# A fused pass with the routed answers added in halves on VectorE, and the gate moved to the next step

## The chip, the cores and the metric

The kernel runs on one core of one Trainium2 chip. The metric is the device time in microseconds of that core, from start to end of one execution; a version is given by the median of its runs. The profile is taken in an execution of its own.

## The reference

The input is 128 graphs of 64 nodes with 256 features, 8192 rows in all. Two layers follow one another, each a graph convolution and a mixture of experts with residuals. The change lies where layer 0 ends and layer 1 begins. Cut to that:

```python
# layer 0, mixture of experts: 64 experts, the best 6 of each row
lattice_out = einsum('bske,bsk->bse', xW, scores)        # sum of 6 weighted answers of a row
proj = lattice_out @ out_w.T + out_b
h = x + proj                                             # x: the normalised row
ffn = (h - mean(h)) * rsqrt(var(h) + 1e-5) * ln_g + ln_b
x = x_before + ffn                                       # x2 in the kernel
# layer 1, graph convolution
h = layer_norm(layernorm(x), ln_gamma, ln_beta)
conv = (adj @ h) @ W_rel + b_rel + h @ W_root
x = x + layernorm(x) + relu(conv)                        # x3 in the kernel
# layer 1, mixture of experts: 8 experts, the best 2 of each row
gate_logits = layernorm(x) @ Wg + bg + bias              # the gate
```

All is in float32; the kernel's tile s holds x + layernorm(x).

## The kernel before

The kernel has four stages: layer 0's convolution and its routing (rows sent to their experts by GpSimd's indirect DMA); layer 0's experts, which send weighted answers to a table in HBM; the fused pass, which reads the six answers of each row back, finishes layer 0, does layer 1's convolution, its gate and its routing; and layer 1's experts.

The fused pass works on blocks of 256 rows (P = 128 partitions, T = 2 tiles of 128 rows, D = 256, K0 = 6 answers, NB = 32 blocks). A helper lays the parts of several blocks one after the other in each step; the pair is a lag and a part, and the part of lag l works on block s - l in step s. Every engine takes its instructions in this order:

```python
        staggered(NB, (
            (-2, load3), (0, layer_out_h), (3, choose1), (-1, mixture), (1, flip_h), (3, count1),
            (2, residual1_a), (0, layer_out_a), (-1, out_proj), (2, residual1_b), (1, neighbours),
            (0, layer_out_b), (1, convolve_a), (2, flip3), (1, convolve_b), (2, gate1), (3, place1),
            (0, layer_out_c), (4, load_w2),
        ))
```

The parts that matter here (cuts marked by ...):

```python
        def load3(b):
            B["y"] = y = work.tile([P, T, K0, D], F32, name="y")          # 2 buffers
            for t in range(T):
                nc.sync.dma_start(out=y[:, t], in_=r0.answer[...])
            # ... xn1, x1, adjacency

        def mixture(b):                       # line 833: sum of 6 answers by accumulating transposes
            pt = psum.tile([P, KD, C], F32, name="ps")
            for t in range(T):
                for k in range(KD):
                    for i in range(K0):
                        nc.tensor.matmul(pt[:, k, ts(t, P)], lhsT=B["y"][:, t, i, ts(k, P)], rhs=ident,
                                         start=(i == 0), stop=(i == K0 - 1), is_transpose=True)
            nc.scalar.copy(accT, pt)          # line 836

        def out_proj(b):                      # line 844: pp = accT.T @ out_wT + out_b
            ...
        def layer_out_h(b):                   # line 850
            nc.vector.tensor_add(h, B["pp"], B["xn1"])

        def layer_out_a(b):
            B["mvh"] = ops.stats(B["h"])      # bn_stats, bn_aggr on VectorE
            B["rsh"] = ops.spread(B["mvh"])   # root on ScalarE
            nc.vector.tensor_add(B["x1"], B["x1"], ln_b...)               # line 856

        def layer_out_b(b):
            nc.vector.reciprocal(rs, rs)
            for t in range(T):                # lines 865 and 867
                nc.vector.scalar_tensor_tensor(h[:, t, :], h[:, t, :], mv[:, t, 0:1], ln_g, subtract, mult)
                nc.vector.scalar_tensor_tensor(x2[:, t, :], h[:, t, :], rs[:, t:t + 1], B["x1"][:, t, :], mult, add)
            B["mv2"] = ops.stats(x2)
            # two roots on ScalarE: std2, rs2

        def layer_out_c(b):                   # VectorE: two reciprocals and shifts; ScalarE: hn (line 884), s
            ...
        def flip_h(b):                        # TensorE turns hn; ScalarE writes hT
        def neighbours(b):                    # TensorE: pz = hT.T @ w_rel; ScalarE copies it to z
        def convolve_a(b), convolve_b(b):     # TensorE: pc = b_rel + hT.T @ w_root, then + at.T @ z

        def residual1_a(b):                   # VectorE: x3 = max(pc, 0) + s, its statistics; ScalarE: root
        def residual1_b(b):                   # VectorE: reciprocal, shift; ScalarE: xs (line 938, written twice wide)
        def flip3(b):                         # TensorE turns xs; ScalarE copies it to xn3T
        def gate1(b):                         # TensorE: pg = xn3T.T @ wg
        def choose1(b):                       # VectorE: logits = pg + bias (line 957), best 2, one-hot
        def count1(b):                        # TensorE: positions from the one-hot
        def place1(b):                        # VectorE: rows of the table; GpSimd: 4 indirect DMAs of xs
```

Of the kernel before, what the change touches and what calls it, by code (L numbers as in the profile page):

```python
# [9 lines left out]
F32 = mybir.dt.float32  # L10
# [5 lines left out]
AF = mybir.ActivationFunctionType  # L16
ALU = mybir.AluOpType
AX = mybir.AxisListType
PSUM = bass.MemoryType.PSUM
P = 128  # L20
# [382 lines left out]
def staggered(n, stages, first=0):  # L403

    for s in range(first + min(lag for lag, _ in stages), n + max(lag for lag, _ in stages)):
        for lag, f in stages:
            if first <= s - lag < n:
                f(s - lag)
# [3 lines left out]
def two_layer_gnn_moe_kernel(ctx: ExitStack, tc: tile.TileContext, a: dict, out: bass.AP):  # L412
    nc = tc.nc
    x_in, adjT = a["x"], a["adjT"]
    N, D = x_in.shape
# [4 lines left out]
    T = 2  # L420
# [5 lines left out]
    K0 = 6  # L426
# [15 lines left out]
    ops = Ops(nc, small, ident, eps)  # L442

    def load_rows(pool, name, engine=nc.scalar):
        t = pool.tile([P, a[name].shape[0]], F32, name="r_" + name)
        engine.dma_start(out=t, in_=rows_of(a[name]))
        return t
# [29 lines left out]
    def by_tile(ap):  # L477
        return ap.rearrange("(t p) d -> p t d", p=P)
# [8 lines left out]
    def load_adjacency(b):  # L487
        at = adjacency[b % 4]
        for g in range(2):
            nc.sync.dma_start(out=at[g * G:(g + 1) * G, :, g * G:(g + 1) * G],  # L490
                              in_=adjT[2 * b * T + g:2 * (b + 1) * T:2].rearrange("t m n -> m t n"))
        return at
# [3 lines left out]
    r0 = Router(tc, const, small, dram, N, D, E0, K0, T, P, 14 * P, 4, "r0")  # L496
# [22 lines left out]
    with tc.tile_pool(name="c0", bufs=1) as c0, \  # L519
# [9 lines left out]
        blocks = [dict() for _ in range(NB)]  # L529
# [263 lines left out]
    with tc.tile_pool(name="c3", bufs=1) as c3, \  # L793
# [5 lines left out]
        ln_g = load_rows(c3, "L0_ffn_ln_g")  # L799
# [11 lines left out]
        blocks = [dict() for _ in range(NB)]  # L811
        pg = pmix.tile([P, T, E1], F32, name="pg")
        r1.begin(counts, work, pmix.tile([P, 2, T, E1], F32, name="pos"))

        def load3(b):
            B = blocks[b]
            B["y"] = y = work.tile([P, T, K0, D], F32, name="y")
            for t in range(T):
                nc.sync.dma_start(out=y[:, t], in_=r0.answer[ts(b * T + t, P * K0), :].rearrange("(p k) d -> p k d", k=K0))
            B["xn1"] = xn1 = work.tile([P, T, D], F32, name="xn1", bufs=3)  # L820
            nc.sync.dma_start(out=xn1, in_=by_tile(xn1_dram[b]))
            B["x1"] = x1 = work.tile([P, T, D], F32, name="x1", bufs=3)
            nc.sync.dma_start(out=x1, in_=by_tile(x1_dram[b]))
            B["at"] = load_adjacency(b)

        def mixture(b):

            B = blocks[b]
            pt = psum.tile([P, KD, C], F32, name="ps")
            for t in range(T):  # L830
                for k in range(KD):
                    for i in range(K0):
                        nc.tensor.matmul(pt[:, k, ts(t, P)], lhsT=B["y"][:, t, i, ts(k, P)], rhs=ident,  # L833
                                         start=(i == 0), stop=(i == K0 - 1), is_transpose=True)
            B["accT"] = accT = work.tile([P, KD, C], F32, name="accT", bufs=1)
            nc.scalar.copy(accT, pt)

# [14 lines left out]
        def layer_out_a(b):  # L852
# [2 lines left out]
            B["rsh"] = ops.spread(B["mvh"])  # L855
            nc.vector.tensor_add(B["x1"], B["x1"], ln_b.unsqueeze(1).to_broadcast([P, T, D]))

        def layer_out_b(b):
            B = blocks[b]
            h = B["h"]  # L860
            mv, rs = B["mvh"], B["rsh"]
            nc.vector.reciprocal(rs, rs)
            B["x2"] = x2 = work.tile([P, T, D], F32, name="x2")
            for t in range(T):
                nc.vector.scalar_tensor_tensor(h[:, t, :], h[:, t, :], mv[:, t, 0:1], ln_g,
                                               op0=ALU.subtract, op1=ALU.mult)
                nc.vector.scalar_tensor_tensor(x2[:, t, :], h[:, t, :], rs[:, t:t + 1], B["x1"][:, t, :],
                                               op0=ALU.mult, op1=ALU.add)
            B["mv2"] = mv = ops.stats(x2)
            B["std2"] = ops.spread(mv)  # L870


            B["rs2"] = rs2 = small.tile([P, T], F32, name="rs2")
            ops.std(rs2, mv[:, :, 1], 1e-10, 1.0 + 1e-5)
# [93 lines left out]
        def place1(b):  # L968
            B = blocks[b]
            r1.send(r1.places(b, B["hot"]), B["xs"])  # L970

        staggered(NB, (
            (-2, load3),
            (0, layer_out_h),
            (3, choose1),
            (-1, mixture),
            (1, flip_h),
            (3, count1),
            (2, residual1_a),
            (0, layer_out_a),  # L980
            (-1, out_proj),
            (2, residual1_b),
            (1, neighbours),
            (0, layer_out_b),
            (1, convolve_a),
            (2, flip3),
            (1, convolve_b),
            (2, gate1),
            (3, place1),
            (0, layer_out_c),  # L990
            (4, load_w2),
# [101 lines left out]
```

## Time and profile before

| | |
|---|---|
| timed runs | 2144.35, 2144.85, 2147.32 us; median 2144.85 us |
| profiled execution, span | 2446.3 us |
| TensorE matmul / weight load busy | 2036.7 us (83%) / 1744.9 us (71%) |
| VectorE, ScalarE, GpSimd busy | 1186.3 us (48%), 1013.6 us (41%), 1157.1 us (47%) |
| fused pass in the profile | about 1480 to 1910 us |
| TensorE / VectorE / ScalarE busy, 1700 to 1800 us | 88.96 / 78.53 / 55.73 us of 100 |
| granted TensorE clock there | 1.00 (0.931 over the whole) |
| DMA share there, and rate | 0.72, 234 GB/s |

PE is TensorE, PEld its weight loads, DVE VectorE, ACT ScalarE, POOL GpSimd and SP SyncE. Shares of the whole span mix four stages; the rows for 1700 to 1800 us are those of the fused pass in its steady part. Busy times of matmuls overlap, since they are pipelined, so that the starts of consecutive matmuls tell their cost better than the durations. The profiled execution is longer than the timed ones by 301 us, which must be kept in mind where a wait is read from the trace.

### The profile page before, as it was taken

How to read it: one execution, taken by the hardware profiler on the slowest of the kernel's cores; microseconds unless marked ns; L12 is line 12 of the kernel's file. 1: busy time of each engine (PE TensorE's matmuls, PEld its weight loads, DVE VectorE, ACT ScalarE, POOL GpSimd, SP SyncE). 2: the span in 40 equal slices, each digit the busy share in tenths (PEclk: the TensorE clock that was granted, in tenths of full speed). 3: DMA queues.
4: the chain of work that ended last, by engine and by line, in shares of the span. 5: the costliest groups of instructions: out<-in, count | busy, mean ns of one | idle time of the engine just before them, and what ended most of it. 6: DMA issues, size and time to landing. Idle time of an engine off the chain costs nothing.

```text
span 2446.3 us, 37355 instructions
## 1 busy us (share of the span) xinstructions
PE 2036.7 (83%) x10564; PEld 1744.9 (71%) x10564; DVE 1186.3 (48%) x3952; ACT 1013.6 (41%) x2037; POOL 1157.1 (47%) x1146
## 2 busy tenths in 40 slices
PE   7888888888884578877878886888888699999998
PEld 6776766767673467766666665777777588888887
DVE  5777776776666322222222234777777222222221
ACT  5766665665662112111111113555555233333332
POOL 0464555455355566666666661333333344444444
PEclk9999989988896799989999998999999799999999
DMA  3233433343236677655555537877773476676665
GB/s 100 90 119 97 132 122 128 123 131 126 88 101 195 199 222 223 203 171 171 178 176 171 146 87 253 300 233 240 232 228 128 141 177 163 156 169 162 161 162 119
DMA packets 284092, 398.93 MB, mean 163 GB/s; under 512 B 56536, under 2 KB 237928, under 8 KB 283888
## 3 DMA queue, kind: packets, MB, share of 16 engines
q1 hardware_dynamic: 204032, 247.67, 34.7%
q0 software_dynamic: 64800, 136.14, 18.7%
q10 hardware_dynamic: 15056, 12.69, 1.6%
q8 instruction: 93, 1.52, 0.3%
q14 instruction: 111, 0.91, 0.1%
HBM read 223.89 MB, written 177.69 MB: 164 GB/s over the span
## 4 chain that ended last, share of the span: by engine, by line
PE 58%; DVE 10%; issue 9%; another core or an unknown queue 8%; ACT 8%; DMA 3%; POOL 2%; SPq 1%; ACTq 0%; POOLq 0%; DVEq 0%
PE py L770 10%; PE ph L1030 9%; PE py L1049 9%; PE ph L599 4%; PE ps L833 3%; PE ps L632 3%; PE pt L755 3%; PE po L844 2%; PE pz L905 2%; PE pc L916 2%; ACT xs L651 2%; ACT lat L602 2%; DVE lat L621 2%; PE ps L76 2%
## 5 line engine op out<-in xcount | busy, mean ns | idle before, releaser
L287 POOL DMA_INDIRECT r0x<-xs,r0row x384 | 390.2, 1016 | 421.0 <-issue 307.1
L770 PE MATMUL py<-lat,pxT 128*128 x1696 | 443.4, 408 | 122.2 <-ACT pxT L757 82.3
L294 POOL DMA_INDIRECT r0y<-py_s,px x424 | 412.5, 973 | 245.9 <-DVE py_s L775 109.9
L770 PEld LDWEIGHTS py<-lat,pxT 128*128 128x128 f32 x1696 | 328.4, 204 | 179.5 <-ACT pxT L757 94.3
L775 DVE TENSOR_SCALAR py_s<-py,px 128x256 f32<-128x256 f32 x424 | 179.5, 478 | 480.0 <-PE py L770 137.8
L302 POOL DMA_INDIRECT out_x<-py_s,px x138 | 214.1, 1551 | 310.1 <-DVE p L1044 124.9
L757 ACT COPY pxT<-pt 128x512 f32<-128x512 f32 x212 | 119.1, 589 | 556.8 <-remote 182.4
L632 PE MATMUL ps<-lat 128*128 128x256 f32 x1024 | 275.7, 420 | 8.3 <-issue 8.0
L1032 ACT ACTIVATE phid<-ph,pw 128x256 f32<-128x256 f32 x276 | 131.0, 475 | 323.8 <-issue 217.4
L632 PEld LDWEIGHTS ps<-lat 128*128 128x128 f32 x1024 | 217.9, 216 | 49.2 <-issue 13.1
L1030 PE MATMUL ph<-pxT,pw 128*128 128x256 f32 x1104 | 252.3, 382 | 0.8 <-ACT pxT L1021 0.8
L1049 PE MATMUL py<-fw,phid 128*128 x1104 | 249.7, 379 | 0.0
L599 PE MATMUL ph<-lat 128*128 128x256 f32 x1024 | 232.8, 386 | 6.8 <-DVE lat L621 6.1
L287 POOL DMA_INDIRECT r1x<-xs,r1row x128 | 126.5, 988 | 226.4 <-DVE bn_rs L881 135.7
L1030 PEld LDWEIGHTS ph<-pxT,pw 128*128 128x128 f32 x1104 | 211.6, 192 | 30.4 <-ACT pxT L1021 1.2
L1049 PEld LDWEIGHTS py<-fw,phid 128*128 128x128 f32 x1104 | 204.5, 190 | 25.0
L599 PEld LDWEIGHTS ph<-lat 128*128 128x128 f32 x1024 | 195.4, 193 | 34.3 <-DVE lat L621 4.8
L755 PE MATMUL pt<-ident,px 128*128 128x128 f32 x848 | 136.3, 285 | 35.4 <-DMA px<-r0x 33.3
L755 PEld LDWEIGHTS pt<-ident,px 128*128 128x128 f32 x848 | 112.5, 148 | 61.9 <-issue 40.5
L602 ACT ACTIVATE lat<-ph,c_L_gnn_b 128x256 f32<-128x256 f32 x256 | 103.9, 470 | 123.4 <-PE ph L599 48.4
L1043 DVE TENSOR_SCALAR p<-p 128x2 f32<-128x2 f32 x69 | 11.9, 173 | 242.3 <-ACT p L1042 238.9
L1052 DVE TENSOR_TENSOR py_s<-py,pb 128x512 f32<-128x512 f32 x69 | 47.7, 692 | 155.6 <-PE py L1049 155.5
(265 smaller groups left out, 2894.5 us busy)
## 6 DMA issues: line engine op xcount, KB each, us to landing
px<-r0x SPq DMA_DIRECT2D x424, 129.0 KB
y<-r0y SPq DMA_DIRECT2D x64, 768.0 KB
pw<-in_L_ffn_W1b SPq DMA_DIRECT2D x69, 514.0 KB
px<-r1x SPq DMA_DIRECT2D x69, 258.0 KB
x<-x SPq DMA_DIRECT2D x64, 256.0 KB
pb<-in_L_ffn_b SPq DMA_DIRECT2D x69, 128.0 KB
r0x<-r0filler ACTq DMA_DIRECT2D x64, 129.0 KB
lat<-in_x SPq DMA_DIRECT2D x32, 256.0 KB
```

Of the source, the lines that this page charges most:

```text
L287: i = self.nc.gpsimd.indirect_dma_start(out=self.table[:, :], out_offset=bass.IndirectOffsetOnAxis(ap=row[:, t, k:k + 1], axis=0), in_=xs[ ...
L294: i = self.nc.gpsimd.indirect_dma_start(out=self.answer[:, :], out_offset=bass.IndirectOffsetOnAxis(ap=x[:, self.D:self.D + 1].bitcast(I32 ...
L302: i, d = f"{self.name}add{i}", self.nc.gpsimd.indirect_dma_start(out=self.total[:, :], out_offset=bass.IndirectOffsetOnAxis(ap=x[:, self.D ...
L599: nc.tensor.matmul(ph[:, c, :], lhsT=w1[:, k, ts(2 * j + c, P)], rhs=B["aggT"][:, k, :], start=(k == 0), stop=(k == KD - 1))
L602: nc.scalar.activation(sq[:, 2 * j + c, :], ph[:, c, :], AF.Square, bias=b1[:, 2 * j + c:2 * j + c + 1], scale=1.0)
L632: nc.tensor.matmul(B["po"][:, t, :], lhsT=B["hT"][:, c, ts(t, P)], rhs=w2[:, c, :], start=False, stop=(t == T - 1 and c == KH - 1))
L755: nc.tensor.transpose(pt[:, k, ts(q, P)], Q["px", q][:, 0, ts(k, P)], ident)
L770: nc.tensor.matmul(py[:, q, :], lhsT=Q["xT"][:, k, ts(q, P)], rhs=lat[:, ds(regs["e"][(2 * j + q) % 4], 1), k, :].rearrange("p o d -> p (o ...
L775: nc.vector.tensor_scalar(y[:, q, :], py[:, q, :], px[:, 0, D + 1:D + 2], None, op0=ALU.mult)
L1030: nc.tensor.matmul(ph, lhsT=w[:, k * F1 + c * P:k * F1 + (c + 1) * P], rhs=Q["xT"][:, k, :], start=(k == 0), stop=(k == KD - 1))
L1032: nc.scalar.activation(hid[:, c, :], ph, AF.Relu, bias=w[:, KD * F1 + c:KD * F1 + c + 1], scale=1.0)
L1049: nc.tensor.matmul(py[:, t, :], lhsT=Q["hid"][:, c, ts(t, P)], rhs=fw2[:, ds(regs["e"][i % 4], 1), c, :].rearrange("p o d -> p (o d)"), st ...
```

## The change

The sum of six answers is formed in two parts: VectorE adds answers 3 to 5 onto answers 0 to 2, in place, two blocks ahead; TensorE's accumulating transposes then run over three instead of six. The load of the answers is a part of its own, one step earlier, with three buffers in place of two. The normalisation of layer 0's output goes from VectorE's fused instructions to two activations of ScalarE, followed on VectorE by one multiplication with ln_g and one addition of x1 for both tiles of rows. The gate's matmuls go from the end of a step to the beginning of the next one; choose follows later on VectorE, after layer_out_a, and count later on TensorE; and in ScalarE's queue the copy that the gate reads stands ahead of the two roots of layer_out_b. The aim is to take transposes from TensorE and to let VectorE's and ScalarE's waits fall together with other work.

```diff
--- before.py
+++ after.py
@@ -812,11 +812,17 @@
         pg = pmix.tile([P, T, E1], F32, name="pg")
         r1.begin(counts, work, pmix.tile([P, 2, T, E1], F32, name="pos"))
 
+        def load_y(b):
+            blocks[b]["y"] = y = work.tile([P, T, K0, D], F32, name="y", bufs=3)
+            for t in range(T):
+                nc.sync.dma_start(out=y[:, t], in_=r0.answer[ts(b * T + t, P * K0), :].rearrange("(p k) d -> p k d", k=K0))
+
+        def halve(b):
+            y = blocks[b]["y"]
+            nc.vector.tensor_add(y[:, :, :K0 // 2, :], y[:, :, :K0 // 2, :], y[:, :, K0 // 2:, :])
+
         def load3(b):
             B = blocks[b]
-            B["y"] = y = work.tile([P, T, K0, D], F32, name="y")
-            for t in range(T):
-                nc.sync.dma_start(out=y[:, t], in_=r0.answer[ts(b * T + t, P * K0), :].rearrange("(p k) d -> p k d", k=K0))
             B["xn1"] = xn1 = work.tile([P, T, D], F32, name="xn1", bufs=3)
             nc.sync.dma_start(out=xn1, in_=by_tile(xn1_dram[b]))
             B["x1"] = x1 = work.tile([P, T, D], F32, name="x1", bufs=3)
@@ -829,9 +835,9 @@
             pt = psum.tile([P, KD, C], F32, name="ps")
             for t in range(T):
                 for k in range(KD):
-                    for i in range(K0):
+                    for i in range(K0 // 2):
                         nc.tensor.matmul(pt[:, k, ts(t, P)], lhsT=B["y"][:, t, i, ts(k, P)], rhs=ident,
-                                         start=(i == 0), stop=(i == K0 - 1), is_transpose=True)
+                                         start=(i == 0), stop=(i == K0 // 2 - 1), is_transpose=True)
             B["accT"] = accT = work.tile([P, KD, C], F32, name="accT", bufs=1)
             nc.scalar.copy(accT, pt)
 
@@ -855,17 +861,19 @@
             B["rsh"] = ops.spread(B["mvh"])
             nc.vector.tensor_add(B["x1"], B["x1"], ln_b.unsqueeze(1).to_broadcast([P, T, D]))
 
+        def layer_out_n(b):
+            B = blocks[b]
+            h = B["h"]
+            rs, nm = ops.scale_shift(B["mvh"], B["rsh"])
+            for t in range(T):
+                nc.scalar.activation(h[:, t, :], h[:, t, :], AF.Identity, bias=nm[:, t:t + 1], scale=rs[:, t:t + 1])
+
         def layer_out_b(b):
             B = blocks[b]
             h = B["h"]
-            mv, rs = B["mvh"], B["rsh"]
-            nc.vector.reciprocal(rs, rs)
             B["x2"] = x2 = work.tile([P, T, D], F32, name="x2")
-            for t in range(T):
-                nc.vector.scalar_tensor_tensor(h[:, t, :], h[:, t, :], mv[:, t, 0:1], ln_g,
-                                               op0=ALU.subtract, op1=ALU.mult)
-                nc.vector.scalar_tensor_tensor(x2[:, t, :], h[:, t, :], rs[:, t:t + 1], B["x1"][:, t, :],
-                                               op0=ALU.mult, op1=ALU.add)
+            nc.vector.tensor_mul(h, h, ln_g.unsqueeze(1).to_broadcast([P, T, D]))
+            nc.vector.tensor_add(x2, h, B["x1"])
             B["mv2"] = mv = ops.stats(x2)
             B["std2"] = ops.spread(mv)
 
@@ -970,22 +978,25 @@
             r1.send(r1.places(b, B["hot"]), B["xs"])
 
         staggered(NB, (
+            (-3, load_y),
             (-2, load3),
+            (3, gate1),
             (0, layer_out_h),
-            (3, choose1),
             (-1, mixture),
             (1, flip_h),
-            (3, count1),
             (2, residual1_a),
             (0, layer_out_a),
+            (3, choose1),
             (-1, out_proj),
             (2, residual1_b),
+            (0, layer_out_n),
             (1, neighbours),
-            (0, layer_out_b),
+            (3, count1),
+            (-2, halve),
             (1, convolve_a),
             (2, flip3),
+            (0, layer_out_b),
             (1, convolve_b),
-            (2, gate1),
             (3, place1),
             (0, layer_out_c),
             (4, load_w2),
```

## The prediction

> **What bounds the kernel now.** I first looked for the stage that the diff touches. The instructions of tile y (the answers that the fused pass reads back) run from 1484 us to 1869 us of the profiled span, so the fused pass takes roughly 1480 to 1910 us of 2446 us. It is cut into steps, one block of 256 rows entering in each; the start of the 24 transposes of line 833 marks a step. The timeline of two stretches gives the step length:
>
> ```profile
> 1512.58 2.78 PE L833 MATMUL ps<-ident,y 128*128 128x128 f32 x24
> ...
> 1515.45 0.59 ACT L836 COPY accT<-ps 128x512 f32<-128x512 f32 x1 [2.01 <-PE ps L833]
> ...
> 1516.09 1.99 PE L844 MATMUL po<-m_L_ffn_out_wT,accT 128*128 128x256 f32 x8
> ```
>
> ```profile
> 1523.78 2.81 PE L833 MATMUL ps<-ident,y 128*128 128x128 f32 x24
> ...
> 1526.69 0.59 ACT L836 COPY accT<-ps 128x512 f32<-128x512 f32 x1 [1.90 <-PE ps L833]
> ...
> 1535.07 2.82 PE L833 MATMUL ps<-ident,y 128*128 128x128 f32 x24
> ...
> 1539.85 0.59 ACT L836 COPY accT<-ps 128x512 f32<-128x512 f32 x1 [3.77 <-PE pos L191]
> ```
>
> ```profile
> 1662.86 2.82 PE L833 MATMUL ps<-ident,y 128*128 128x128 f32 x24
> ...
> 1667.15 0.59 ACT L836 COPY accT<-ps 128x512 f32<-128x512 f32 x1 [3.29 <-PE pos L191]
> ...
> 1667.79 1.99 PE L844 MATMUL po<-m_L_ffn_out_wT,accT 128*128 128x256 f32 x8 [1.36 <-ACT accT L836]
> ```
>
> Columns: start us, duration, engine and line, tiles, and in brackets the idle time before it and what ended it. Read the first column. In the first two steps shown TensorE goes from one mixture to the next in 11.20 us (1512.58 to 1523.78) and 11.29 us (1523.78 to 1535.07), almost without waiting: the copy of the mixture starts 0.1 us after the last transpose ends. Later (1650.16, 1662.86, 1675.53) a step takes 12.7 us, and the difference is one wait: the copy starts some 1.4 us after the transposes end (1665.68), and TensorE stands for it. The wait appears with the step of 1535 us, the first in which GpSimd sends rows by indirect DMA. The waits of the stretch 1500 to 1868 us, 29 steps, say the same (waiter, what it waited for, us in total, times, longest):
>
> ```profile
> ACT accT L836 <- PE pos L191: 86.9, 26, 3.8
> ...
> PE po L844 <- ACT accT L836: 37.5, 27, 1.8
> ...
> DVE logits L957 <- PE pg L951: 29.8, 25, 1.4
> ...
> DVE bn_rs L67 <- ACT bn_sd L36: 21.1, 27, 1.3
> ```
>
> Nothing in the program makes this copy wait for more than its transposes. The profiled execution took 2446 us and the timed ones 2145 us, so some 300 us of what the trace shows is absent from the timed runs. I take this late signal to belong to it (chance 0.8): in a timed run **TensorE bounds the fused pass at about 11.25 us a step**, and VectorE is close behind. All waits of VectorE in that stretch, with the small ones, come to 57.4 us, or 1.98 us a step, so it is occupied 12.68 - 1.98 = **10.7 us a step**, of which 11.25 leaves about half a microsecond.
>
> **What the Trainium skill says.** "VectorE: DVE Perf Modes", section "The perf-mode tier table": an fp32 tensor_tensor runs at one element a cycle only; section "The TRN2 errata" gives (N+151)/0.96 ns, 691 ns for 512 elements. The trace agrees: 659 ns with both inputs in SBUF (line 856), 691 ns with one in PSUM (line 850). "Perfetto Trace Analysis", section "Per-engine timelines", says that a matmul's end is modelled from its size; so I trust starts, and the 1.4 us rests on the copy's start as well. "TensorE: Matmul & The Clock Gate", section "PE-mode transpose", says that transposes don't count as TensorE work to the clock gate in the same way; the clock was 1.00 in this stretch with 32 transposes a step, so no run here shows what thinner work does.
>
> **The change, part by part.** The rows that carry the costs (groups of 1540 to 1868 us; the numbers behind the bar are busy us and mean ns of one):
>
> ```profile
> L833 PE MATMUL ps<-ident,y 128*128 128x128 f32 x617 | 72.5, 274 | 0.0
> ...
> L938 ACT ACTIVATE xs<-x,bn_nm,bn_rs 128x512 f32<-128x512 f32 x52 | 39.6, 810 | 7.7 <-issue 6.2 <-POOL xs L249 1.2 <-DVE bn_nm L68 0.2
> ...
> L884 ACT ACTIVATE hn<-x,bn_nm,bn_rs 128x256 f32<-128x256 f32 x52 | 28.3, 594 | 0.0
> ...
> L867 DVE SCALAR_TENSOR_TENSOR x<-h,bn_sd,x 128x256 f32<-128x256 f32 x52 | 25.2, 485 | 1.8
> ...
> L865 DVE SCALAR_TENSOR_TENSOR h<-h,bn_mv,r_L_ffn_ln_g 128x256 f32<-128x256 f32 x52 | 24.6, 473 | 0.0
> ...
> L856 DVE TENSOR_TENSOR x<-x,r_L_ffn_ln_b 128x512 f32<-128x512 f32 x26 | 17.1, 659 | 0.0
> ```
>
> - TensorE: 12 of 24 transposes go. 24 take 2.65 us start to start (1662.86 to 1665.51), so this is -1.32 us a step. TensorE without its waits goes from some 11.1 to 9.8 us.
> - VectorE, halving: one add of 1536 elements. From the 659 ns of 512 and one element per cycle of 0.96 GHz (the clock on the "VectorE: DVE Perf Modes" page, section "Specifications") I estimate 659 + 1024/0.96 = 1726 ns, and 1.64 us of occupation, because an independent instruction starts some 0.08 us before the end of the one ahead of it (as at line 867 to 865).
> - VectorE, output norm: four instructions of 473 and 485 ns (1.83 us start to start, 1656.55 to 1658.38) become a multiply and an add of 512, dependent on each other, 2 x 0.69 = 1.38 us, and one 0.16 us instruction for the shift. Together VectorE gets +1.64 - 1.83 + 1.38 + 0.2 = +1.4 us: **12.1 us of occupation**, above TensorE's 11.25.
> - ScalarE: two activations of 256, 1.09 us a step as at line 884 (pair). It has room, but they stand behind the two of line 938 in its queue.
> - Gate at the next step's begin: choose no longer waits for it (1.2 us a step in the profile, half of that in a step of 11.25). In the new order choose, 1.58 us, stands between the statistics and the reciprocals and so covers the roots (0.73 us).
> - The third buffer and earlier load of y: the same bytes; TensorE waited for y only in the first steps (22 us in 7 waits), so worth little.
>
> Then a new wait. VectorE's multiply needs h from ScalarE. In VectorE's order the shift of x3 releases the two activations of line 938 (1.52 us for the pair, of which the second lets go after 0.70 us each, 1.40 us) and behind them the two new ones (1.08 us); with two handovers h is ready 2.6 us after that shift. VectorE meanwhile has 0.3 us of small work and the halving, some 1.95 us, and stands 0.65 us. A step along VectorE, from starts in the step of 1662.86 us: h add 0.61; x3, two sets of statistics and the x1 add 3.44; choose 1.58; reciprocal and shift 0.36; until h is there 2.61; multiply and add 1.38; statistics of x2 1.08; places, reciprocals and shifts 1.71. The sum is **12.77 us**. The length of the halving doesn't enter; it lies within the 2.61.
>
> **The total.** 12.77 - 11.25 = +1.5 us a step. It applies where choose, norm and mixture all run, about 29 of 36 steps: +43 us. In the first steps, without choose and place, VectorE has 2.5 us less and the new kernel may gain up to a microsecond each; say -2 us. 2145 + 41 = 2186 us. I shade it to 2182 for the rival.
>
> **Rivals.**
> 1. The late signal is real in timed runs also. Then the step before is 12.68 us, VectorE's 12.77 us replaces it and the late copy falls into TensorE's new slack: +3 us, about 2148. For it: it recurs in every step. Against it: the 300 us between profile and timing have to be somewhere, and the same kind of late TensorE signal is seen in the stages with the most GpSimd sends. Chance 0.2.
> 2. TensorE's relief is what counts and VectorE keeps up: a step of about 10 us, -35 us. The 10.7 us of VectorE before the change and the +1.4 us speak against it; it needs the fp32 add at twice its rate and no wait for h. Chance 0.02.
> 3. TensorE, with 3 us of idle time in each step, is granted a lower clock, and its chain from hn over hT, pz and z to pc gets longer than the slack of about 0.7 us; a few tenths a step more, 2190 to 2200. No idle stretch above 1.5 us is expected, so a minor share.
> 4. DMA: its share of 0.72 at 12.68 us is about 0.81 at 11.25 us, so the pass before may be somewhat slower than 11.25 us in timed runs; then the loss shrinks by a few us.
>
> **Range and chances.** The first reading gives 2176 to 2197, the first rival 2140 to 2155. A range for 8 in 10 must hold both: 2142 to 2198. Slower by over 2% starts at 2187.7, about the middle of the main case with the third rival added: 0.43. Faster by over 2% needs rival 2 in full: 0.02. Within 2% is left with 0.55.
>
> **What the profile after would show.** VectorE's halving at about 1.73 us; its waits for logits and roots nearly gone, and one for h of about 0.65 us before the multiply; TensorE idle some 3 us a step; the step in the profile about 12.7 to 12.8 us, hardly other than before, so that the profiled span stays near 2446 us while the timed runs grow. If the profiled step stays and the timed runs stay too, the late signal was no matter of profiling and rival 1 holds. If the halving takes clearly less than 1.7 us, my rate for it is wrong, without effect on the step. The prediction fails most if VectorE has no wait for h, or if the timed step before is not 11.25 us.

## The result and the profile after

The changed kernel takes **2201.07 us** (four runs, 2198.19 to 2203.2), the kernel before in the same comparison 2144.6 us (2143.31 to 2147.32). The ratio is 1.0261, 95% interval 1.0243 to 1.0279: the change costs 56.5 us. The profiled execution of after has a span of 2201.4 us, as long as its timed runs, so its trace can be read without correction. TensorE's matmuls are busy for 1921.6 us (2036.7 before), VectorE 1231.6, ScalarE 1044.1, GpSimd 1162.8 us: TensorE is busy 115 us less, and the kernel is slower.

On some of the chips used the kernel before takes about 2484 us, with TensorE's signals coming late as in the profile of before, and on the others about 2147 us as in the timed runs, so each experiment is compared only with the kernel before on its own chip. I call them late chips and prompt chips.

First a step of after, in the timeline (VectorE and a few lines of the others; start us, duration):

```profile
1403.35 1.52 ACT L946 ACTIVATE xs<-x,bn_nm,bn_rs 128x512 f32<-128x512 f32 x2 [2.12 <-DVE bn_rs L67]
1403.45 1.76 DVE L822 TENSOR_TENSOR y<-y 128x1536 f32<-128x1536 f32 x1
1404.77 1.07 ACT L869 ACTIVATE h<-h,bn_nm,bn_rs 128x256 f32<-128x256 f32 x2
1405.88 0.69 DVE L875 TENSOR_TENSOR h<-h,r_L_ffn_ln_g 128x512 f32<-128x512 f32 x1 [0.67 <-ACT h L869]
...
1408.15 1.51 PE L839 MATMUL ps<-ident,y 128*128 128x128 f32 x12
...
1416.29 1.76 DVE L822 TENSOR_TENSOR y<-y 128x1536 f32<-128x1536 f32 x1
...
1420.99 1.51 PE L839 MATMUL ps<-ident,y 128*128 128x128 f32 x12
```

From halving to halving (1403.45 to 1416.29) and from mixture to mixture (1408.15 to 1420.99) it is **12.84 us**. VectorE stands once in a step: after the halving it waits 0.67 us for h, because ScalarE first writes the two halves of xs (1403.35) and only then h (1404.77). The waits of the stretch 1240 to 1600 us say the same (waiter, awaited, us in total, times, longest):

```profile
PE ps L76 <- ACT hn L892: 22.4, 47, 2.5
...
DVE h L875 <- ACT h L869: 18.0, 27, 0.9
```

No wait for logits is left, and that for roots is 3.8 us in 5 times. TensorE now waits for others in every step. In 1400 to 1500 us (us, busy times of PE, PEld, DVE, ACT, POOL, clock, DMA share, GB/s) VectorE is the fullest engine:

```profile
1400.00:1500.00 100.00, 85.90 (x491) 70.28 (x489) 88.36 (x346) 60.47 (x131) 31.41 (x38) 0.97 0.71 231
```

The other part is the beginning of the pass. Its timeline in after:

```profile
1213.36 0.34 SPq L818 DMA_DIRECT2D y<-r0y  x1
...
1230.02 0.17 DVE L808 TENSOR_TENSOR r_L_ffn_bg<-r_L_ffn_bg,r_L_ffn_bias 128x8 f32<-128x8 f32 x1 [15.17 <-DMA r_L_ffn_bias<-in_L_ffn_bias]
...
1230.77 3.43 DVE L822 TENSOR_TENSOR y<-y 128x1536 f32<-128x1536 f32 x2 [0.51 <-DMA y<-r0y]
...
1232.63 2.79 PE L839 MATMUL ps<-ident,y 128*128 128x128 f32 x12 [48.69 <-DMA xn<-xn]
```

and in the profile of before:

```profile
1478.31 0.34 SPq L819 DMA_DIRECT2D y<-r0y  x1
...
1484.05 2.79 PE L833 MATMUL ps<-ident,y 128*128 128x128 f32 x12 [17.28 <-DMA y<-r0y]
...
1491.98 0.17 DVE L808 TENSOR_TENSOR r_L_ffn_bg<-r_L_ffn_bg,r_L_ffn_bias 128x8 f32<-128x8 f32 x1 [11.63 <-DMA r_L_ffn_bias<-in_L_ffn_bias]
```

Before, the first mixture starts 5.7 us after the first load of answers is issued, and the tiny addition of the gate's bias (line 808), which waits for a transfer, comes later and holds up nothing. After, the first mixture starts 19.3 us after the load: it needs the halving, the halving stands behind line 808 in VectorE's queue, and line 808 waits 15.17 us for its bias. Line 808 starts 16.7 us after the load of answers, in before 13.7 us; why the bias comes later isn't shown.

### The profile page after: what moved, and what is told of

Read it like the earlier page. It is cut to its first block, busy times and chain, and to the rows that moved or that the text cites. A ratio compares the mean times of both kernels' runs of the same rounds, so it can differ in the third digit from the quotient of the medians.

```text
span 2201.4 us, 36751 instructions
## 1 busy us (share of the span) xinstructions
PE 1921.6 (87%) x10180; PEld 1649.8 (75%) x10180; DVE 1231.6 (56%) x3952; ACT 1044.1 (47%) x2101; POOL 1162.8 (53%) x1146
## 3 DMA queue, kind: packets, MB, share of 16 engines
q10 hardware_dynamic: 15056, 12.69, 1.8%
## 4 chain that ended last, share of the span: by engine, by line
DMA 32%; PE 25%; DVE 21%; POOL 8%; issue 8%; ACT 6%; ACTq 0%; SPq 0%; POOLq 0%; DVEq 0%
DMA r0y<-py_s,px 17%; PE py L1060 8%; PE ph L1041 8%; POOL r0x L287 6%; DMA out_x<-py_s,px 5%; DVE bn_st L45 3%; DMA r0x<-xs,r0row 3%; DMA r1x<-xs,r1row 3%; PE py L770 2%; DVE lat L609 2%; DMA px<-r0x 2%; PE ph L599 2%; DVE lat L621 2%; ACT xs L946 1%; DVE bn_mv L46 1%
## 5 line engine op out<-in xcount | busy, mean ns | idle before, releaser
L287 POOL DMA_INDIRECT r0x<-xs,r0row x384 | 395.6, 1030 | 256.4 <-issue 171.7
L770 PE MATMUL py<-lat,pxT 128*128 x1696 | 409.6, 385 | 40.3 <-DVE py_s L775 23.6
L775 DVE TENSOR_SCALAR py_s<-py,px 128x256 f32<-128x256 f32 x424 | 185.6, 480 | 362.3 <-PE py L770 150.8
L770 PEld LDWEIGHTS py<-lat,pxT 128*128 128x128 f32 x1696 | 306.7, 191 | 90.4 <-ACT pxT L757 32.7
L757 ACT COPY pxT<-pt 128x512 f32<-128x512 f32 x212 | 123.8, 585 | 429.7 <-PE pt L755 281.1
L632 PE MATMUL ps<-lat 128*128 128x256 f32 x1024 | 237.6, 381 | 0.0
L632 PEld LDWEIGHTS ps<-lat 128*128 128x128 f32 x1024 | 193.4, 191 | 24.4
L755 PE MATMUL pt<-ident,px 128*128 128x128 f32 x848 | 127.9, 274 | 37.1 <-DMA px<-r0x 37.1
L755 PEld LDWEIGHTS pt<-ident,px 128*128 128x128 f32 x848 | 106.4, 142 | 58.5 <-issue 37.3
L623 ACT ACTIVATE lat<-lat,c_L_gnn_rms_weight 128x256 f32<-128x256 f32 x256 | 105.6, 495 | 36.9 <-DVE lat L621 36.5
```

Source lines behind the costliest of these rows:

```text
L287: i = self.nc.gpsimd.indirect_dma_start(out=self.table[:, :], out_offset=bass.IndirectOffsetOnAxis(ap=row[:, t, k:k + 1], axis=0), in_=xs[ ...
L632: nc.tensor.matmul(B["po"][:, t, :], lhsT=B["hT"][:, c, ts(t, P)], rhs=w2[:, c, :], start=False, stop=(t == T - 1 and c == KH - 1))
L755: nc.tensor.transpose(pt[:, k, ts(q, P)], Q["px", q][:, 0, ts(k, P)], ident)
L757: nc.scalar.copy(xT[:, :, :n * P], pt[:, :, :n * P])
L770: nc.tensor.matmul(py[:, q, :], lhsT=Q["xT"][:, k, ts(q, P)], rhs=lat[:, ds(regs["e"][(2 * j + q) % 4], 1), k, :].rearrange("p o d -> p (o ...
L775: nc.vector.tensor_scalar(y[:, q, :], py[:, q, :], px[:, 0, D + 1:D + 2], None, op0=ALU.mult)
```

## The experiments

My theory after this reading had two parts: the step is VectorE's queue with its wait for h (12.84 us against 11.3 us before on a prompt chip), and the bias delays the beginning. The rivals were that the step before is 12.7 us in timed runs too, so that the loss lies elsewhere; that the halving itself sets the step; and that the changed place of the gate does.

### What the step before is in a timed run

The kernel before, unchanged, was profiled again on two late chips (three executions):

> The kernel before, profiled once more. Theory A (the late TensorE signals of the first profile belong to that execution and not to the timed runs): the span falls to about the timed 2145 us, the copy of the mixture starts 0.1 us after its last transpose, and a step of the fused pass takes 11.2 to 11.3 us. Theory B (the late signal is part of the program): the step stays at 12.7 us and the span near 2446 us.

> The kernel before once more, profiled, hoping for an execution in which TensorE's signals are not late (the earlier run of it took 2473 us and showed them again). Theory A: where the whole takes about 2145 us, the copy of the mixture starts 0.1 us after its last transpose and a step of the fused pass takes 11.2 to 11.3 us. Theory B: the step is 12.7 us there also.

> The kernel before, profiled, complete with its sends. Theory A: where it takes about 2145 us, the step is 11.29 us as without the sends, and between 2470 and 2490 us it is 12.8 us.

They took 2472.93, 2480.26 and 2480.65 us and have steps of 12.79, 12.78 and 12.78 us. The waits of the second, 1560 to 1900 us:

```profile
ACT accT L836 <- PE pos L191: 78.4, 23, 3.5
```

ScalarE stands 3.4 us a step ahead of the copy. In the step of 1704.84 us the next matmul starts at 1707.49 us, so the transposes are through by about then, and the copy starts at 1709.21 us, 1.7 us later; the program doesn't make it wait for the matmul named, line 191. So the late copy of the mixture is the same as in the first profile. The timed runs on these chips are as long as the profiled ones (medians of 2483.86, 2484.27 and 2482.17 us), so the late copy belongs to the chip or its condition, not to profiling. It is the smaller part of what a late chip costs: the first answers are loaded at 1495.6 to 1504.5 us there and at 1212.9 us on a prompt chip (e8, below), so that 283 to 292 of the 337 us arise ahead of the fused pass, in stages that no run here changed.

The traces tie the late copy to GpSimd's sends. In the profile of before and in these three, it starts 0.1 us after the transposes in the two steps ahead of the first send, and in each of 107 later steps it starts 0.8 to 1.3 us after the end of the last of the step's four sends. One step with sends has no late copy, that of 1577.80 us in e1b: its last send ends at 1579.52 us, 1.1 us before its transposes do. It and the next step, in the timeline of e1b (DMA_INDIRECT is a send, the fourth of its step):

```profile
1578.55 0.97 POOL L287 DMA_INDIRECT r1x<-xs,r1row  x1 [0.31 <-issue]
...
1580.71 0.59 ACT L836 COPY accT<-ps 128x512 f32<-128x512 f32 x1 [1.90 <-PE ps L833]
...
1591.93 0.97 POOL L287 DMA_INDIRECT r1x<-xs,r1row  x1 [0.30 <-issue]
...
1593.98 0.59 ACT L836 COPY accT<-ps 128x512 f32<-128x512 f32 x1 [3.88 <-remote]
```

To find whether the sends cause it, the sends of layer 1's rows were left out of the kernel before and of after. Both then leave out layer 1's experts' real input and read filler rows instead; the work of the other engines stays.

```diff
-            r1.send(r1.places(b, B["hot"]), B["xs"])
+            r1.places(b, B["hot"])
...
-            r1.fetch(i, row, x)
+            nc.sync.dma_start(out=x, in_=r1.table[ds(r1.spare, r1.pg), :].rearrange("(t p) d -> p t d", p=P))
```

> The kernel before without GpSimd's sends of the fused pass; layer 1's experts then read the page of fillers, so that their part is left out of the output. TensorE's late signals went with GpSimd's sends in the traces so far. Theory A: without sends there is no late signal in the fused pass on any chip, and its full step, choose and place included, takes 11.2 to 11.3 us. Theory B: the 12.7 us belong to the step, and it stays there.

> The changed kernel without GpSimd's sends of the fused pass, layer 1's experts on fillers, as in the run beside it. Theory A with C: the step is set by VectorE and ScalarE, 12.8 us with sends and without, so 1.5 to 1.6 us longer than that of the kernel before without sends. Theory B: both are at 12.7 to 12.8 us.

> The changed kernel itself, timed beside the kernel before on whatever chip this call gets. Theory A: where the kernel before takes about 2145 us, ratio 1.026; where it takes about 2484 us, its step is 12.8 us as the changed one's and only the beginning (some 10 us) is lost, ratio 1.003 to 1.007. Theory B: ratio 1.026 there also.

> The kernel before without GpSimd's sends of the fused pass, layer 1's experts on fillers, once more. On a chip where the kernel before takes 2484 us: Theory A, the late signals of the fused pass go with the sends and its step falls from 12.8 to 11.3 us. Rival: they come from something else, such as the loads, and the step stays at 12.8 us. On a chip where it takes 2145 us: 11.29 us again.

All four ran on prompt chips, where the kernel before takes 2148.15 and 2149.81 us. Without sends, before took 2176.21 and 2183.69 us and after 2232.0 us (one execution each; from the last hn to the end they take 588 us and more, against 560 in after, and in that stage they read the fillers). After unchanged took 2203.96 us, ratio 1.0263 (1.0246 to 1.028). So whether a late chip without sends has no late copy was not tested. But e8 and g1 show what I had wanted more, the step before without late signals, 11.29 us in every full step. A stretch of the timeline of e8:

```profile
1395.94 2.82 PE L833 MATMUL ps<-ident,y 128*128 128x128 f32 x24
...
1398.85 0.59 ACT L836 COPY accT<-ps 128x512 f32<-128x512 f32 x1 [1.90 <-PE ps L833]
...
1407.24 2.82 PE L833 MATMUL ps<-ident,y 128*128 128x128 f32 x24
```

The copy follows the transposes at once and TensorE doesn't wait for it; from 1265 to 1590 us TensorE is busy for 321.26 of 325 us. After has 12.73 us without and 12.83 us with sends, and the difference e9 - e8 is 55.8 us, the same as the change costs with its sends in both kernels (55.8 us, 2203.96 - 2148.15). That the sends add little to the step before on a prompt chip follows from this agreement, to within several us only, since g1 took 7.5 us more than e8; a trace of it with sends on a prompt chip wasn't taken.

The loss is therefore located with e8 against after, and with e8 against e9, where both are without sends. The tile hn, written once for each block at the end of its output norm, gives the first and last start (duration min/median/max, first to last start):

```profile
L884 ACT ACTIVATE hn<-x,bn_nm,bn_rs x64: 584/594/604, 1240.3 to 1586.8; 128x256 f32<-128x256 f32 x64
```

```profile
L892 ACT ACTIVATE hn<-x,bn_nm,bn_rs x64: 582/593/608, 1248.1 to 1641.7; 128x256 f32<-128x256 f32 x64
```

The first answers are loaded at 1212.9 us in e8 and at 1213.4 us in after, which gives

| us | first load to first hn | first to 4th hn | 4th to 32nd hn | chip |
|---|---|---|---|---|
| before without sends (e8) | 27.4 | 30.4 | 315.6 | prompt |
| after | 34.7 | 33.6 | 359.5 | prompt |
| difference | +7.3 | +3.2 | +43.9 | |
| after without sends (e9) | 35.6 | 34.1 | 356.7 | prompt |
| difference of e9 and e8 | +8.2 | +3.7 | +41.0 | |

Together +54.4 of 56.5 us; about 2 us lie elsewhere. Without sends in either it is +52.9 of 55.5 us between the profiled spans; the rest is 1.3 us ahead of the first load and 1.2 us behind the last hn. So the full steps cost 41 to 44 us. The first column is the least certain: g1, the same kernel as e8, has 29.1 us there. The last of the three steps in the second column is a full one, since the first choose runs in it (1273.35 us in after): it takes 12.69 us in after and 11.30 us in e8, so that 1.4 of the 3.2 us belong to the full steps, 29 in all.

### The bias of the gate moved out of the way

```diff
-        nc.vector.tensor_add(bg, bg, gbias)
...
         def choose1(b):
+            if b == 0:
+                nc.vector.tensor_add(bg, bg, gbias)
```

> The changed kernel, with the addition of the two gate biases moved from ahead of the fused pass to its first choose. Theory P (at the beginning the first halving stands in VectorE's queue behind this addition, which waits 15 us for the DMA of a bias, and TensorE waits for the halving): the fourth mixture comes some 8 to 11 us earlier, the time falls from 2201 to about 2191 us, steps unchanged at 12.84 us. Rival Q (the first mixture is late because three blocks of answers share the DMA engines): no change, 2200 us.

> The changed kernel with the bias addition late. The first profile of it showed the fourth mixture 7 us sooner after the first load of answers than in the changed kernel. Theory P: 7 us less than the changed kernel, ratio about 1.023 where the kernel before takes 2145 us. Rival Q (those 7 us are given back later): ratio 1.026.

On two late chips: 1.0032 (1.0019 to 1.0045) and 1.0031 (1.0013 to 1.005), step 12.84 us. The beginning, in the timeline of e2:

```profile
1505.90 0.34 SPq L817 DMA_DIRECT2D y<-r0y  x1
...
1515.11 1.76 DVE L821 TENSOR_TENSOR y<-y 128x1536 f32<-128x1536 f32 x1 [7.65 <-DMA m_L_gnn_W_root<-in_L_gnn_W_root]
...
1516.97 2.79 PE L838 MATMUL ps<-ident,y 128*128 128x128 f32 x12 [19.17 <-DMA m_L_ffn_Wg<-in_L_ffn_Wg]
```

The first halving starts 9.2 us after the load of answers in place of 17.4, the first mixture 11.1 in place of 19.3, and the fourth 38.1 in place of 45.4 us: 7 us are kept. Line 808 is their cause, and rival Q (no change) is out. After was traced on a prompt chip and e2 on a late one, but e11 below, on a prompt chip, has 11.1 and 39.0 us too. Of the rest of the delay of the first mixture (11.1 less the 5.7 of before), nearly all goes with the halving (next experiment, 6.3 us). What the 7 us are worth in a timed run wasn't measured on one chip: after wasn't timed on a late chip, nor e2 on a prompt one. These ratios mustn't be held against 1.0261, since the kernel before is held up by its late copy on these chips.

### Six transposes again, no halving

```diff
-                    for i in range(K0 // 2):
+                    for i in range(K0):
-                                         start=(i == 0), stop=(i == K0 // 2 - 1), is_transpose=True)
+                                         start=(i == 0), stop=(i == K0 - 1), is_transpose=True)
...
-            (-2, halve),
```

> The changed kernel without the halving: TensorE transposes six answers again, all else as changed. Theory C (a step is set by the chain of VectorE through ScalarE's xs and h, in which the halving lies hidden): VectorE loses 1.64 us of work a step and the step still takes 12.7 to 12.8 us, its wait for h growing from 0.67 to about 2.4 us; the time falls only by what the beginning gives back, to some 2190 us. Rival D (VectorE's load is what counts, and the halving is the added load): the step falls to about 11.2 to 11.5 us and the time to 2150 to 2155 us.

> The changed kernel without the halving. Its steps were 12.84 us in the first profile of it. Theory C: the time falls only at the beginning and end, 8 to 14 us under the changed kernel, ratio 1.020 to 1.023 where the kernel before takes 2145 us. Rival D (load): ratio 1.005.

> The changed kernel without the halving, once more, for a chip where the kernel before takes 2145 us. Theory C: ratio 1.020 to 1.023 there. Rival D (load): ratio 1.005. Elsewhere 1.002 again.

Late chips: 1.0005 (0.9989 to 1.0021) and 1.0021 (1.0009 to 1.0033). Prompt chip: 2193.2 us, **1.0207** (1.019 to 1.0224). The step is 12.84 us on both, exactly that of after, although VectorE has 1.76 us less work and TensorE 12 more transposes. The timeline of g2:

```profile
1398.54 0.69 DVE L875 TENSOR_TENSOR h<-h,r_L_ffn_ln_g 128x512 f32<-128x512 f32 x1 [2.35 <-ACT h L869]
...
1400.81 2.81 PE L839 MATMUL ps<-ident,y 128*128 128x128 f32 x24
...
1413.64 2.82 PE L839 MATMUL ps<-ident,y 128*128 128x128 f32 x24
```

The wait for h grew from 0.67 to 2.35 us, by what the halving had filled. The granted clock is 1.00 in 1400 to 1500 us, against 0.97 in after, so the clock doesn't make the step either. In after the halving is free; undoing it gains only at the beginning. There the first mixture starts 6.3 us after the load, and the first hn comes 25.6 us after it (34.7 in after): 9.1 us of some 11 us (2193.2 against 2203.96 us for after in another comparison on a prompt chip).

### The norm ahead of xs in ScalarE's queue

If the wait for h is the second part of the loss, putting the two activations of the output norm ahead of those of xs removes it, and VectorE's own work is left.

```diff
-            (2, residual1_b),
             (0, layer_out_n),
+            (2, residual1_b),
```

> The changed kernel with the normalisation of layer 0's output ahead of the two wide activations of xs, on VectorE and ScalarE. Theory C: the wait of 0.67 us for h goes, and with it 0.7 to 0.9 us of each step, which takes 11.9 to 12.2 us; 29 steps make 19 to 26 us, so about 2175 to 2182 us. Rival D (load alone): the load is the same, so no change, 2200 us.

> The changed kernel with both mends: norm of layer 0's output ahead of xs, bias addition late. Steps of 12.08 us and 7 to 10 us less at the beginning: some 30 us below the changed kernel. Where the kernel before takes about 2145 us that is still above it, ratio 1.011 to 1.014; where it takes 2484 us, ratio 0.991 to 0.995.

e4, on a late chip: 0.9961 (0.9946 to 0.9975), step 12.08 us. e11, with the bias moved as well, on a prompt chip: 2172.08 us, 1.0122 (1.01 to 1.0143), step 12.07 us; it is 32 us faster than after in the same comparison. The timeline of e4:

```profile
1709.72 1.09 ACT L869 ACTIVATE h<-h,bn_nm,bn_rs 128x256 f32<-128x256 f32 x2 [2.19 <-DVE bn_rs L67]
1709.82 1.76 DVE L822 TENSOR_TENSOR y<-y 128x1536 f32<-128x1536 f32 x1
...
1711.50 0.69 DVE L875 TENSOR_TENSOR h<-h,r_L_ffn_ln_g 128x512 f32<-128x512 f32 x1
...
1723.57 0.69 DVE L875 TENSOR_TENSOR h<-h,r_L_ffn_ln_g 128x512 f32<-128x512 f32 x1
```

The multiplication follows the halving without a wait, and from one to the next it is 12.07 us: now VectorE is hardly ever idle (0.9 us in all, from 1560 to 1900 us), and this is its occupation. In e11 the first hn comes 27.5 us after the load, as before the change (27.4), and first to last hn take 370.7 us (393.6 in after): 7.2 + 22.9 us, nearly the whole 32. TensorE needed 11.29 us with 12 transposes more, so VectorE is the bound now; and as 12.07 us is above 11.29 us, this form of the change doesn't win on a prompt chip. No run has the norm first and no halving, which would show whether TensorE's 11.29 us would then limit the step again.

### The output norm back on VectorE

Only the halving, the earlier load and the gate's place are left of the change; layer_out_n is taken out and layer_out_b is the old one.

```diff
-            nc.vector.tensor_mul(h, h, ln_g.unsqueeze(1).to_broadcast([P, T, D]))
-            nc.vector.tensor_add(x2, h, B["x1"])
+            for t in range(T):   # the two scalar_tensor_tensor of before, after nc.vector.reciprocal(rs, rs)
...
-            (0, layer_out_n),
```

> The changed kernel with layer 0's output norm back on VectorE in its four fused instructions; halving, gate and queue order as changed. Theory C: the wait for h is gone, VectorE's chain is 0.61 + 3.44 + 1.58 + 0.36 + 0.08 + 1.64 + 1.83 + 1.08 + 1.71 = 12.3 us, so a step of 12.2 to 12.4 us against 12.84; over 29 steps some 15 us less than the changed kernel, so about 1.9% above the kernel before where that takes 2145 us. Rival (the gain of the norm's move outweighs its wait): a step above 12.84 us.

> The changed kernel with the norm back on VectorE. Its steps were 12.25 us in the first profile of it: 29 times 0.59 us less than the changed kernel, with the first steps some 20 us, ratio 1.016 to 1.018 where the kernel before takes 2145 us.

Late chips: 0.9961 (0.9946 to 0.9977) and 0.9976 (0.9963 to 0.9989), steps 12.25 and 12.24 us. VectorE stands 0.7 us in all from 1560 to 1900 us in e5, so this too is its occupation. Moving the norm to ScalarE therefore made the step 0.6 us longer in the order of after, and 0.17 us shorter with the norm first. It wasn't run on a prompt chip; by its step, 12.25 against 11.29 us, I would expect it above before there, but no run shows it.

### The gate's place alone, and the halving on GpSimd

The kernel before with the stage order of the gate, choose and count from after:

```diff
+            (3, gate1),
-            (3, choose1),
-            (3, count1),
             (0, layer_out_a),
+            (3, choose1),
...
-            (0, layer_out_b),
+            (3, count1),
             (1, convolve_a),
             (2, flip3),
+            (0, layer_out_b),
             (1, convolve_b),
-            (2, gate1),
```

> The kernel before with only the new order: gate at the next step's begin, choose after layer_out_a, the gate's copy ahead of the roots of layer_out_b; no halving, the norm as before, two buffers of answers. Theory C: TensorE's load is unchanged at 11.1 us, VectorE's 10.7 us; a step of 11.1 to 11.3 us, a ratio of 0.995 to 1.003 where the kernel before takes 2145 us. Rival (the order itself costs, because choose and the copy delay the roots): a step of 11.6 us or more, ratio above 1.005.

On a late chip: 1.0000 (0.9984 to 1.0016), step 12.78 us. The late copy of the mixture still sets the step there (TensorE waits for it 37.4 us in 25 times from 1560 to 1900 us), so this tells nothing of a prompt chip; whether the order alone gains or loses there isn't shown. The waits of VectorE were exchanged, not removed: for logits they are gone, and those for the two roots come to 50.2 us in 32 times in that stretch. In after the waits for logits and roots are nearly gone, but choose, 1.59 us, now stands on VectorE ahead of the shift that releases xs and so h. Its place is thus a part of the chain that leads to the wait for h, and no run moves it alone out of after; with that wait gone (e4) the step is 12.08 us all the same.

The halving on GpSimd, with the norm of before and the bias moved:

```diff
-            nc.vector.tensor_add(y[:, :, :K0 // 2, :], y[:, :, :K0 // 2, :], y[:, :, K0 // 2:, :])
+            nc.gpsimd.tensor_add(y[:, :, :K0 // 2, :], y[:, :, :K0 // 2, :], y[:, :, K0 // 2:, :])
```

> The changed kernel with the halving given to GpSimd, the norm back on VectorE and the bias addition late. GpSimd is busy for a third of the stage; VectorE's load is then 10.7 us and TensorE's 9.8 us. Theory C: if GpSimd adds 1536 elements in under 5 us and does not slow VectorE, a step of 10.5 to 10.9 us and a ratio of 0.98 to 0.99 against the kernel before of 2145 us. Rival: GpSimd's adds are so slow, or take so much of VectorE's time at the memory, that the step is 11.5 us or more.

On a late chip: 1.0017 (0.9999 to 1.0035), with a median step of 12.26 us but a mean of 12.95 us; the 10.5 to 10.9 us of theory C are missed, as its rival said. GpSimd's addition takes 3433 ns. VectorE loses what it gave away; its groups in 1560 to 1900 us (busy us, mean ns of one):

```profile
L861 DVE TENSOR_TENSOR x<-x,r_L_ffn_ln_b 128x512 f32<-128x512 f32 x26 | 45.3, 1744 | 0.0
...
L181 DVE CAST r1which<-r1idx 128x4 f32<-128x4 uint32 x26 | 31.5, 1210 | 0.9
```

In e5 the same two take 658 and 170 ns. In e7 itself, the 16 additions of line 861 that overlap one of GpSimd's take 2421 ns in the mean and the other 10 take 661 ns; of the conversions, 9 overlap and take 3173 ns, and 17 don't and take 170 ns.

## Why the prediction was wrong

The prediction said 2182 us and 2142 to 2198 us for 8 in 10; 2201.07 us lies 3 us above the range. The mechanism was right: the step is VectorE's queue with its wait for h. What was mis-sized is the term for the first steps.

- **The step before, 11.25 us:** 11.29 us without sends on prompt chips. Right.
- **VectorE's sum, 12.77 us:** 12.84 us. In the trace of after the terms are, from h's addition: 0.60, 3.43, 1.59, 0.36, 2.61, 1.45, 1.09, 1.71. Only the multiplication and addition differ, 1.45 in place of 1.38 us: each takes 0.69 us, but the one that needs the other's result starts 0.73 us after it (1405.88 and 1406.61). The wait for h is 0.67 us (0.65 said).
- **"The length of the halving doesn't enter":** shown by g2, whose step without any halving is 12.84 us. The halving takes 1758 ns by the median of 32, against the 1726 of the estimate, which started from the 659 ns of line 856; (1536+151)/0.96 of the Trainium skill, "VectorE: DVE Perf Modes", section "The TRN2 errata", gives 1757 ns.
- **VectorE's occupation, 12.1 us:** 12.08 and 12.07 us, in e4 and e11 where the wait is gone.
- **+43 us from the full steps:** +43.9 us over 28 steps and +1.4 us in one more; without sends in either kernel 41.0 and 1.4. Right.
- **"In the first steps ... say -2 us":** this is the step that failed. The traces have +9.1 us there: 7.3 us until the first hn (5.6 us against g1) and 1.8 us in the next two steps. I had counted what VectorE has to do in these steps and not where the first halving stands in its queue: behind an addition whose operand arrives late. Both could be seen beforehand: the 11.63 us wait of line 808 in the profile of before, and the halving's place behind it in the listing. e2 and e11 show 7 us to be that: in e11 the first hn comes 27.5 us after the load, in before 27.4. The sentence that the load of y was "worth little" looked at TensorE's wait for y (22 us in 7 waits) and missed that the halving needs every half of y ahead of the first transpose. The two steps behind it are no shorter in g2 and e11 (21.6 and 21.2 us against 20.9 in after and 19.1 in e8), so neither the halving, nor the bias, nor the norm's place in the queue makes them longer; the cause stays open.
- **Shading by 4 us, and the low end of the range:** they served rival 1, the late signal as a matter of timed runs also. Rival 1 is a fact on late chips and isn't one where the kernel is timed at 2145 us. The reason given against it, that the signal belongs to the profiled execution, was wrong, since late chips have it in timed runs as well; that the timed runs of 2145 us are free of it was right, and with it the 11.25 us. The same error made the forecast that the profiled span would stay near 2446 us: it is 2201.4 us. Without the shading and with the right beginning the same sum is 2145 + 43 + 9.1 = 2197.1 us.
- **Rival 2** (VectorE keeps up) falls with g2 and e11. **Rival 3:** the clock did go down, from 1.00 to 0.97 in the stretch 1400 to 1500 us, and TensorE's waits in the step from 1408.15 us are 0.78 + 0.17 + 0.69 + 0.63 = 2.3 us (3 said), but g2 at 1.00 has the same step of 12.84 us. **Rival 4** (DMA slows the step before) isn't seen in e8, whose sends are left out and whose DMA share is 0.62; with sends it wasn't tested.

## What to carry to other kernels

Before work is moved to another engine, write down that engine's queue from end to end, waits included: the step was predicted within 0.07 us in this way, and a halving that costs nothing in a full step cost 7 us once, since its first instance stood behind an unrelated instruction waiting for a transfer. An in-order queue makes the first steps of a pipeline a case of their own: look for what a newly critical engine still waits for there. Where the profiled execution is longer than the timed ones, find what the extra time is made of before choosing which of its waits to believe.

## What the runs showed of the hardware

- The same kernel takes about 2147 us on some chips and 2484 us on others, 16% more. In the fused pass the difference of a step is the copy that starts about 1.5 us after the transposes end (11.29 and 12.78 us). So the verdict on a change depends on the chip: the order with the norm first, whose step is 12.07 to 12.08 us on both, is 0.4% faster than before on a late chip and, with the bias moved, 1.2% slower on a prompt one. After itself wasn't timed on a late chip. On late chips the late copy goes with GpSimd's sends (it starts 0.8 to 1.3 us after the end of the last of them); why on these chips alone stays open. The profile of before, with its 2446 us, looks like one from a late chip, and which chip it was isn't known.
- An addition of 1536 fp32 elements takes GpSimd 3433 ns and VectorE 1758 ns. The Trainium skill, "GPSIMD Engine Reference", section "Instruction dispatch", gives approximately 2.5 cycles an element as the floor for two inputs, at its 1.2 GHz an estimate of 3200 ns; the trace lies 7% above it. Its section "Specifications" says that GpSimd's access to SBUF is shared with VectorE, with contention where VectorE has two SBUF inputs or a two-port mode. The runs agree: VectorE's addition, with both inputs in SBUF, takes 661 ns where it doesn't overlap a GpSimd addition and 2421 ns in the mean where it does; a conversion of four elements goes from 170 to 3173 ns.
